# A macaron block (MoE, local attention, MoE): the experts' queues are no longer filled beforehand, and the first block's turning and the weights' splitting are moved

## The chip, the cores and the metric

The kernel runs on one core of one Trainium2 chip. A core has five engines, each with its own in-order list of instructions: TensorE (PE, matrix products, its weight loads shown as PEld), VectorE (DVE), ScalarE (ACT), GpSimd (POOL) and SyncE (SP, which here only issues transfers). Engines wait for one another, and for transfers, by semaphores; an instruction that waits holds up everything behind it on its engine. Sixteen DMA engines move data between DRAM and the on-chip memories SBUF and PSUM. The metric is the device time of one execution in microseconds, as the median of several runs.

## The reference

4096 tokens (2 x 2048) of width 256 go through three residual steps:

```
x = x + 0.5 * ffn(layernorm(x))
x = x + attention(layernorm(x))
x = x + 0.5 * ffn(layernorm(x))

def ffn(x):                             # 8 experts, 2 per token
    xn = x * rsqrt(mean(x*x) + eps)
    probs = softmax(xn @ router_w.T)
    topk_p, topk_i = top_k(probs, 2);  rw = topk_p / sum(topk_p)
    capacity = int(1.25 * 4096 / 8)     # 640
    # each expert takes its first 640 tokens, in the order of tokens
    dispatch = argsort(~sel, axis=1, stable=True)[:, :capacity]
    valid = arange(capacity) < count
    eout = (silu(xg @ rg) * (xg @ ru)) @ rd          # inner width 1024
    routed = zeros.at[dispatch].add(eout * (w * valid))
    shared = (silu(x @ sg) * (x @ su)) @ sd          # inner width 2048
    return shared + routed
```

The attention is causal within groups of 64 tokens, with 16 heads of width 16 and an RMS norm on q and k. With two experts per token the mean queue would be 1024 tokens long, so a queue of 640 places usually overflows, and tokens beyond its end are dropped.

## The kernel before

**Numbers in two halves.** Each product is made of three float16 products: value and weight are split into a high and a low half, and the lo x lo term is left out (`TERMS`). `split` (L97) makes the halves of a weight: a cast on ACT, then a subtraction on DVE. `two` (L161) does it for tokens.

**Four phases.** Phase a handles the tokens of the first ffn in 32 tiles of 128 (`tile1`): load y, statistics, normalise to z (`planes`, L146), write both halves into a row buffer X (ten of them), transpose into xb, compute router logits, and after each fourth tile route a block of 512 tokens (`route`, L214). Between these steps the shared expert is computed for blocks 0 to 4: `shared` (L349) goes through 16 chunks of the inner width, each with gate and up products (L306) into three PSUM buffers pgu, a Silu on ACT (L317), products on DVE (sl, L319), the halves hh (ACT, L321) and hl (DVE, L322), and the down products (L330), which are deferred past the next chunk's gate and up. Phase b computes the experts of the first ffn, phase c the rest of the first shared expert, the attention, and the second shared expert, and phase d the experts of the second ffn.

**Queues in DRAM.** `scatter` (L279) writes X, with a tag of token number and weights, by indirect transfers from POOL into the place that the token has in its expert's queue xg. Before that, `fill` (L742) writes zeros and a token number outside the range to all places: a memset on POOL, a small write on DVE and a transfer of 650 KB for each expert and each ffn, sixteen in all. All scatters of one ffn wait for its fills.

**Experts.** `experts` (L389) goes through 8 experts, with 8 chunks of weights each. For each chunk it loads re and re2, splits them into wc and wd, and computes gate and up for two stretches of columns, 384 and 256. `expert_load` (L373) brings the next expert's tokens (a transposing transfer) and tags; from the tag it makes eid, the token numbers as integers (a copy on POOL, L384), and ew, the weights (DVE, L385 and L387). After an expert's last chunk, `fin` scales the five tiles of output into eo, on DVE and ACT in turn, and POOL issues five indirect transfers that add them to the output rows named by eid (L426). They run while the next expert's first chunks are computed. eid, ew and tag have two buffers each, so those of expert e+2 take the place of those of expert e, and wait until its readers are done: for eid these are the five indirect transfers.

**What sets the order.** The program is written as generators: `drive` takes one step of the shared expert after another and lets the tiles take their steps in between; `run_slots` lets only the tiles run. The order in which the framework then lays the instructions out on each engine comes from a planner that simulates times while the program is built, so an edit can move instructions that it does not name. On the chip that order is fixed. SP issues nearly all plain and transposing transfers, one after another.

In phase a the first block is turned on TensorE (`turn`, L177), since no transposing transfer has to be waited for there; `front_steps` (L606) holds this. `load_shared` (L118) loads the shared expert's weights in eight pairs of chunks and splits them, all at one point of the program, after the first block's tiles.

Of the kernel before, what the change touches and what calls it, by code (L numbers as in the profile page):

```python
# [20 lines left out]
P = 128  # L21
# [8 lines left out]
E = 8  # L30
# [7 lines left out]
class Net:  # L38
    def __init__(self, ctx, tc):
# [27 lines left out]
        nc.gpsimd.memset(self.e1, 2.718281828459045)  # L67
        tk = self.sm.tile([P, 32], I32, name="tk", bufs=1)
# [35 lines left out]
    def load_router(self, router_w):  # L104
        nc = self.nc
        r = self.raw.tile([E, H], F32, name="rtr", tag="raw2")
# [11 lines left out]
    def load_shared(self, sg, su, sd):  # L118
# [5 lines left out]
        for c in range(0, 16, 2):  # L124
            r = self.raw.tile([P, 2, 2, 2 * P], F32, name=f"rs{c}", tag="raw")
            for i, s in enumerate((sg, su)):
                nc.sync.dma_start(
                    out=r[:, i], in_=s[:, c * P:(c + 2) * P].rearrange("(k p) f -> p k f", p=P))
            for j in range(2):
                src = r[:, :, :, j * P:(j + 1) * P]  # L130
                self.split(self.sgu[:, c + j, 0], self.sgu[:, c + j, 1], src)
            r2 = self.raw.tile([P, 2, H], F32, name=f"rd{c}", tag="raw2")
            nc.sync.dma_start(out=r2, in_=sd[c * P:(c + 2) * P].rearrange("(k p) f -> p k f", p=P))
            self.split(self.sdw[:, 0, c:c + 2], self.sdw[:, 1, c:c + 2], r2)

# [10 lines left out]
    def planes(self, x, xp, mv, rstd, pool=False):  # L146

        nc = self.nc
        z = self.tok.tile([P, H], F32, name="z", bufs=3)
# [8 lines left out]
        self.two(xp, z, pool)  # L158
# [55 lines left out]
    def route(self, R, b, fb):  # L214
# [33 lines left out]
        nc.vector.tensor_tensor(out=R["run"], in0=C[:, 3, :], in1=M[:, 3, :], op=ALU.add)  # L248
        yield
# [24 lines left out]
        for t in range(4):  # L274
            with self.tc.issue_after(self.anchor.ins) if self.anchor else nullcontext():
                self.scatter(R, b, fb, t, di, w1, dl, ef)
            yield

# [94 lines left out]
    def expert_load(self, R, e, hold):  # L373
# [10 lines left out]
        nc.gpsimd.tensor_copy(ids, tag[:, :, 0])  # L384
# [88 lines left out]
    def attn_tile(self, R, j, x2, new_fb):  # L473
# [12 lines left out]
        self.planes(y, xa, mv, rstd, True)  # L486
# [119 lines left out]
    def front_steps(self, y, t, new_fb, keep=None):  # L606
# [6 lines left out]
        z = self.planes(y, xp, fb["mv"][:, t, :], fb["rstd"][:, t:t + 1], keep is not None)  # L613
        xt = fb["xb"][:, :, t * P:(t + 1) * P]
        if fb["pe"]:
            self.turn(z, xt)
            fb["n"] += 1
            for _ in range((3 - t) * GAP_A + 1):
                yield
        if keep is not None:  # L620
# [16 lines left out]
class Tiles:  # L637
# [12 lines left out]
    def steps(self):  # L650
# [17 lines left out]
        self.slot += 1  # L668

# [27 lines left out]
def macaron(ctx, tc, x, w_qkv, ln_w, w_proj, router_w, rg, ru, rd, sg, su, sd, out):  # L697
# [24 lines left out]
    def tile1(j):  # L722
# [3 lines left out]
        yield  # L726
        yield from n.front_steps(y, t, new_fb(1, b))
# [14 lines left out]
    def fill(R):  # L742

        for e in range(E):
            z = n.raw.tile([P, 5, XW], F32, name="zero")
            nc.gpsimd.memset(z, 0.0)
            nc.vector.tensor_scalar_add(z[:, :, H], n.tokid[:, 0:5], float(T + e * CAP))
            nc.sync.dma_start(out=R["xg"][e * CAP:(e + 1) * CAP].rearrange("(t p) f -> p t f", p=P), in_=z)
            yield

# [75 lines left out]
```

## Time and profile before

| What | Value |
|---|---|
| Median of 3 runs | 1871.48 us (1870.2 to 1871.99) |
| Profiled execution, its own time | 1875.79 us |
| Its span in the profile | 1874.1 us |
| Granted TensorE clock, mean | 0.994 |
| Instructions | 37396 |
| Transfers | 196.07 MB, mean 105 GB/s |

In the profile a row of the time order has start, duration, engine, line, operation, output<-inputs, size, and in brackets the idle time before it with what ended it. A row of groups has busy time and mean duration, and the idle time ahead. A row of waits has who waited for whom, total us, times and the longest. TensorE's busy time counts matmuls from issue to modelled end, and neighbours overlap: in the experts' phases six matmuls of 128 x 384 take 0.98 us. The costliest lines are these:

```profile
L306 PE MATMUL pgu<-xb,sgu 128*128 128x512 f16 x3072 | 738.8, 380 | 26.3 <-DVE sl L319 11.1
L306 PE MATMUL pgu<-xe,wc 128*128 128x384 f16 (+1 forms) x3072 | 497.0, 299 | 0.5
L426 POOL DMA_INDIRECT out_dram<-eo,eid x40 | 64.6, 1616 | 313.8 <-DVE hl L322 248.3
L287 POOL DMA_INDIRECT xg<-X,di x128 | 136.0, 1063 | 112.2 <-DVE di L266 54.1
```

### The profile page before, as it was taken

To read this page: it belongs to the slowest core of one execution; us is meant where nothing else is said; L and a number is where in the kernel's file an instruction comes from. 1 tells how busy PE (TensorE), PEld (TensorE's weight loads), DVE (VectorE), ACT (ScalarE), POOL (GpSimd) and SP (SyncE) were. 2 spreads that over 40 slices of the span, in tenths; PEclk is the share of its full clock that TensorE was granted. 3 is DMA by queue.
4 is the path that set the end of the run, shared out by engine and by line. 5 is a ranking of instruction groups with operands and counts; after the bars stand their busy time and mean duration, and the time that the engine had idled before them with its cause. 6 is when DMAs were issued, how large, how long until landed. Compare 5 with 4: busy or idle time off the path is not lost.

```text
span 1874.1 us, 37396 instructions
## 1 busy us (share of the span) xinstructions
PE 1786.8 (95%) x13546; PEld 1191.7 (64%) x13546; DVE 1262.5 (67%) x3190; ACT 942.1 (50%) x1991; POOL 724.5 (39%) x943
## 2 busy tenths in 40 slices
PE   6899999999999999999999999999999999999996
PEld 3455555677777765666565655656566567777775
DVE  8756554456666656788888888888886556565663
ACT  5323323355555535666566666656643335555553
POOL 5743332011112223455757667575753001111122
PEclk9999999999999999999999999999999999999998
DMA  9742113045455424556657576766631304544542
GB/s 278 220 125 75 35 29 86 21 102 115 112 113 125 104 55 86 110 105 120 139 114 141 102 141 119 135 121 119 129 62 37 86 12 102 114 113 105 117 109 50
DMA packets 447481, 196.07 MB, mean 105 GB/s; under 512 B 302353, under 2 KB 444365, under 8 KB 447248
## 3 DMA queue, kind: packets, MB, share of 16 engines
q1 hardware_dynamic: 429632, 172.51, 41.1%
q0 software_dynamic: 17664, 21.17, 6.6%
q8 instruction: 106, 1.74, 0.4%
q14 instruction: 79, 0.65, 0.1%
HBM read 80.52 MB, written 52.33 MB: 71 GB/s over the span
## 4 chain that ended last, share of the span: by engine, by line
PE 57%; DVE 12%; POOL 10%; issue 9%; DMA 6%; ACT 4%; SPq 2%; POOLq 0%; DVEq 0%; ACTq 0%
PE pgu L306 36%; PE po L330 19%; POOL xg L287 3%; DVE hl L322 2%; DVE sl L319 2%; DVE sl L314 2%; DMA xg<-X,di 1%; DMA QT<-QK 1%; DMA rs<-in_L_ffn_su_dram 1%; POOL X L285 1%; DMA y<-in_L_attn_x_dram 1%; ACT hh L321 1%; POOL e L561 1%; DVE st L139 1%; POOL S L550 1%
## 5 line engine op out<-in xcount | busy, mean ns | idle before, releaser
L306 PE MATMUL pgu<-xb,sgu 128*128 128x512 f16 x3072 | 738.8, 380 | 26.3 <-DVE sl L319 11.1
L321 ACT CAST hh<-sl 128x512 f16<-128x512 f32 (+2 forms) x512 | 272.8, 533 | 563.3 <-DVE sl L319 521.4
L306 PE MATMUL pgu<-xe,wc 128*128 128x384 f16 (+1 forms) x3072 | 497.0, 299 | 0.5
L306 PEld LDWEIGHTS <-sgu 128*128 128x128 f16 x3072 | 293.2, 98 | 301.1 <-issue 35.8
L319 DVE SCALAR_TENSOR_TENSOR sl<-pgu,sl 128x512 f32<-128x512 f32 (+2 forms) x512 | 300.2, 587 | 204.7 <-PE pgu L306 171.4
L322 DVE TENSOR_TENSOR hl<-sl,hh 128x512 f16<-128x512 f32 (+2 forms) x512 | 328.4, 642 | 154.4 <-ACT hh L321 147.5
L330 PEld LDWEIGHTS <-hh 128*128 128x128 f16 x3328 | 320.6, 98 | 115.0 <-ACT hh L321 17.9
L306 PEld LDWEIGHTS <-wc 128*128 128x128 f16 x3072 | 300.5, 98 | 94.1 <-issue 1.8
L330 PE MATMUL po<-sdw,hh 128*128 128x256 f16 x2048 | 351.9, 273 | 7.3 <-ACT hh L321 6.9
L330 PE MATMUL po<-sdw,hl 128*128 128x256 f16 x1024 | 251.9, 274 | 15.8 <-DVE hl L322 10.8
L330 PE MATMUL po<-wd,hh 128*128 128x256 f16 x1280 | 223.4, 273 | 0.0
L330 PEld LDWEIGHTS <-hl 128*128 128x128 f16 x1664 | 162.9, 98 | 67.4 <-DVE hl L322 27.2
L317 ACT ACTIVATE sl<-pgu 128x384 f32<-128x384 f32 (+1 forms) x336 | 159.0, 473 | 55.3 <-PE pgu L306 34.2
L426 POOL DMA_INDIRECT out_dram<-eo,eid x40 | 64.6, 1616 | 313.8 <-DVE hl L322 248.3
L287 POOL DMA_INDIRECT xg<-X,di x128 | 136.0, 1063 | 112.2 <-DVE di L266 54.1
L426 POOL DMA_INDIRECT acc<-eo,eid x40 | 65.1, 1627 | 285.4 <-DVE hl L322 245.8
L330 PE MATMUL po<-wd,hl 128*128 128x256 f16 x640 | 152.4, 273 | 2.1 <-DVE hl L322 2.1
L314 DVE SCALAR_TENSOR_TENSOR sl<-sl,pgu 128x512 f32<-128x512 f32 x176 | 119.9, 681 | 38.3 <-ACT sl L313 37.2
L100 ACT ACTIVATE wc<-re 128x512 f16<-128x512 f32 x128 | 80.5, 629 | 83.3 <-PE pgu L306 52.9
L313 ACT ACTIVATE sl<-pgu 128x512 f32<-128x512 f32 x176 | 103.9, 591 | 33.3 <-PE pgu L306 31.8
L101 DVE SCALAR_TENSOR_TENSOR wc<-re,wc 128x512 f16<-128x512 f32 x128 | 88.3, 690 | 26.6 <-ACT wc L100 26.4
L550 POOL TENSOR_TENSOR S<-S,amx 128x1024 f32<-128x1024 f32 x32 | 63.7, 1990 | 81.3 <-DVE amx L549 74.4
(140 smaller groups left out, 1719.6 us busy)
## 6 DMA issues: line engine op xcount, KB each, us to landing
re<-in_L_ffn_rg_dram SPq DMA_DIRECT2D x128, 128.0 KB
re<-in_L_ffn_ru_dram SPq DMA_DIRECT2D x128, 128.0 KB
re<-in_L_ffn_rd_dram SPq DMA_DIRECT2D x128, 128.0 KB
xg<-zero SPq DMA_DIRECT2D x16, 650.0 KB
y<-acc SPq DMA_DIRECT2D x64, 128.0 KB
y<-in_L_attn_x_dram SPq DMA_DIRECT2D x32, 128.0 KB
acc<-xr SPq DMA_DIRECT2D x16, 256.0 KB
x<-y SPq DMA_DIRECT2D x32, 128.0 KB
```

The costliest lines, as they stand in the source:

```text
L101: nc.vector.scalar_tensor_tensor(out=lo, in0=src, scalar=WS, in1=hi, op0=ALU.mult, op1=ALU.subtract)
L287: i = nc.gpsimd.indirect_dma_start(out=R["xg"][:, :], out_offset=bass.IndirectOffsetOnAxis(ap=di[:, t, k:k + 1], axis=0), in_=X, in_offset ...
L306: nc.tensor.matmul(p, lhsT=wc[:, w, i, k, :], rhs=x[:, 2 * a + k, :], start=(j == 0), stop=(j == 5))
L313: nc.scalar.activation(s, p, AF.Tanh, scale=0.5 / XP)
L314: nc.vector.scalar_tensor_tensor(out=s, in0=s, scalar=1.0, in1=p, op0=ALU.add, op1=ALU.mult)
L317: nc.scalar.activation(s, p, AF.Silu, scale=1.0 / XP)
L319: nc.vector.scalar_tensor_tensor(out=s, in0=ps[1], scalar=1.0 / XP / (2.0 * XP if tanh else 1.0), in1=s, op0=ALU.mult, op1=ALU.mult)
L321: nc.scalar.copy(h[0], s)
L322: nc.vector.tensor_tensor(out=h[1], in0=s, in1=h[0], op=ALU.subtract)
L330: nc.tensor.matmul(o, lhsT=h[a][:, t * P:(t + 1) * P], rhs=wd[:, w], start=(c == 0 and j == 0 and t % 2 == 0), stop=(c == nch - 1 and j == 2),
L426: i = nc.gpsimd.indirect_dma_start(out=R["acc"][:, :], out_offset=bass.IndirectOffsetOnAxis(ap=ids[:, t:t + 1], axis=0), in_=eo, in_offset ...
L550: self.anchor = nc.gpsimd.tensor_tensor(out=S, in0=S, in1=mx.unsqueeze(2).to_broadcast([P, 16, 64]), op=ALU.subtract)
```

## The change

- `fill` is gone for both ffns. Places that no token took hold whatever the memory held. After the last block is routed, `limits` sums the queues' counts over all partitions with one matmul, and makes two small tables: a mask of bits and an offset for each place of each queue. In `expert_load`, eid is made on DVE: the tag's bits are masked, and 8192 is added for places that were not taken, so that the adding transfer skips them. The copy on POOL is gone.
- `acc` for blocks 5 to 7 is no longer copied from x in DRAM by three transfers of 512 KB; each tile's y is written from SBUF, 128 KB at a time.
- `planes` is divided into `normed` and `two`. In the first block, the turning comes first and `two` (the halves for the scatter) later. z has five buffers instead of three.
- The shared expert's weights have four buffers of each kind instead of two. Their loads and splits are written as a generator: the first pair is loaded at the start, from ACT's queue, and split when the first block is ready; the others are loaded and split one pair in every six steps of the first block (`fed`).
- A small Silu at the start loads ACT's function table.
- `load_router`'s buffer is its own.

```diff
--- before.py
+++ after.py
@@ -65,6 +65,8 @@
         nc.gpsimd.memset(self.mhalf, -0.5)
         self.e1 = c.tile([P, 4], F32, name="e1")
         nc.gpsimd.memset(self.e1, 2.718281828459045)
+        warm = c.tile([P, 8], F32, name="warm")
+        nc.scalar.activation(warm, self.mhalf, AF.Silu)
         tk = self.sm.tile([P, 32], I32, name="tk", bufs=1)
         nc.gpsimd.iota(tk, pattern=[[P, 32]], base=0, channel_multiplier=1)
         self.tokid = c.tile([P, 32], F32, name="tokid")
@@ -103,7 +105,7 @@
 
     def load_router(self, router_w):
         nc = self.nc
-        r = self.raw.tile([E, H], F32, name="rtr", tag="raw2")
+        r = self.raw.tile([E, H], F32, name="rtr", bufs=1)
         nc.sync.dma_start(out=r, in_=router_w)
         self.rwt = self.cst.tile([P, 2, 2 * E], F16, name="rwt")
         p = self.m1([P, 2, E], F32, "prt")
@@ -122,16 +124,20 @@
         self.sgu = w.tile([P, 16, 2, 2, 2, P], F16, name="sgu")
         self.sdw = w.tile([P, 2, 16, H], F16, name="sdw")
         for c in range(0, 16, 2):
-            r = self.raw.tile([P, 2, 2, 2 * P], F32, name=f"rs{c}", tag="raw")
+            issue = nc.sync if c else nc.scalar
+            r = self.raw.tile([P, 2, 2, 2 * P], F32, name=f"rs{c}", tag="raw", bufs=4)
             for i, s in enumerate((sg, su)):
-                nc.sync.dma_start(
+                issue.dma_start(
                     out=r[:, i], in_=s[:, c * P:(c + 2) * P].rearrange("(k p) f -> p k f", p=P))
+            r2 = self.raw.tile([P, 2, H], F32, name=f"rd{c}", tag="raw2", bufs=4)
+            issue.dma_start(out=r2, in_=sd[c * P:(c + 2) * P].rearrange("(k p) f -> p k f", p=P))
+            if c == 0:
+                yield
             for j in range(2):
                 src = r[:, :, :, j * P:(j + 1) * P]
                 self.split(self.sgu[:, c + j, 0], self.sgu[:, c + j, 1], src)
-            r2 = self.raw.tile([P, 2, H], F32, name=f"rd{c}", tag="raw2")
-            nc.sync.dma_start(out=r2, in_=sd[c * P:(c + 2) * P].rearrange("(k p) f -> p k f", p=P))
             self.split(self.sdw[:, 0, c:c + 2], self.sdw[:, 1, c:c + 2], r2)
+            yield
 
     def stats(self, x, mv, rstd):
         nc = self.nc
@@ -143,10 +149,10 @@
             out=ve, in0=mv[:, 1:2], scalar1=LN_EPS, scalar2=1.0 / UP ** 2, op0=ALU.add, op1=ALU.mult)
         nc.gpsimd.tensor_tensor(out=rstd, in0=ve, in1=self.mhalf[:, :1], op=ALU.pow)
 
-    def planes(self, x, xp, mv, rstd, pool=False):
-
-        nc = self.nc
-        z = self.tok.tile([P, H], F32, name="z", bufs=3)
+    def normed(self, x, mv, rstd, pool=False):
+
+        nc = self.nc
+        z = self.tok.tile([P, H], F32, name="z", bufs=5)
         if pool:
             nm = self.sm.tile([P, 1], F32, name="nm")
             nc.vector.scalar_tensor_tensor(
@@ -155,7 +161,6 @@
         else:
             nc.vector.tensor_scalar(
                 out=z, in0=x, scalar1=mv[:, 0:1], scalar2=rstd, op0=ALU.subtract, op1=ALU.mult)
-        self.two(xp, z, pool)
         return z
 
     def two(self, xp, z, pool=False):
@@ -246,6 +251,9 @@
         for t in range(3):
             nc.vector.tensor_tensor(out=C[:, t + 1, :], in0=C[:, t, :], in1=M[:, t, :], op=ALU.add)
         nc.vector.tensor_tensor(out=R["run"], in0=C[:, 3, :], in1=M[:, 3, :], op=ALU.add)
+        if b == NB - 1:
+            yield
+            self.limits(R)
         yield
         pp = self.m1([P, 4, E], F32, "pp")
         nc.tensor.matmul(pp, lhsT=self.tri, rhs=M, start=True, stop=False)
@@ -275,6 +283,21 @@
             with self.tc.issue_after(self.anchor.ins) if self.anchor else nullcontext():
                 self.scatter(R, b, fb, t, di, w1, dl, ef)
             yield
+
+    def limits(self, R):
+
+        nc = self.nc
+        p = self.m1([P, E], F32, "pn")
+        nc.tensor.matmul(p, lhsT=self.ones, rhs=R["run"], start=True, stop=True)
+        taken = self.sm.tile([P, E, 5], F32, name="taken", bufs=1)
+        nc.vector.tensor_tensor(
+            out=taken, in0=self.tokid[:, 0:5].unsqueeze(1).to_broadcast([P, E, 5]),
+            in1=p.unsqueeze(2).to_broadcast([P, E, 5]), op=ALU.is_lt)
+        R["bits"] = self.cst.tile([P, E, 5], I32, name=R["key"] + "b")
+        nc.vector.tensor_scalar_mul(R["bits"], taken, -1.0)
+        R["off"] = self.cst.tile([P, E, 5], F32, name=R["key"] + "o")
+        nc.vector.tensor_scalar(
+            out=R["off"], in0=taken, scalar1=-8192.0, scalar2=8192.0, op0=ALU.mult, op1=ALU.add)
 
     def scatter(self, R, b, fb, t, di, w1, dl, ef):
         nc = self.nc
@@ -381,7 +404,9 @@
         yield
         ids = hold["id"] = self.sm.tile([P, 5], I32, name="eid")
         w = hold["w"] = self.sm.tile([P, 5], F32, name="ew")
-        nc.gpsimd.tensor_copy(ids, tag[:, :, 0])
+        tk = self.sm.tile([P, 5], I32, name="tkb")
+        nc.vector.tensor_tensor(out=tk, in0=tag[:, :, 0].bitcast(I32), in1=R["bits"][:, e], op=ALU.bitwise_and)
+        nc.vector.tensor_tensor(out=ids, in0=tk.bitcast(F32), in1=R["off"][:, e], op=ALU.add)
         nc.vector.scalar_tensor_tensor(
             out=w, in0=tag[:, :, 3], scalar=float(e), in1=tag[:, :, 1], op0=ALU.is_equal, op1=ALU.mult)
         nc.vector.tensor_tensor(out=w, in0=w, in1=tag[:, :, 2], op=ALU.add)
@@ -483,7 +508,7 @@
         self.stats(y, mv, rstd)
         yield
         xa = a.tile([P, 2 * H], F16, name="xa")
-        self.planes(y, xa, mv, rstd, True)
+        self.two(xa, self.normed(y, mv, rstd, True), True)
         yield
         V2 = self.V2[j % 2]
         xt = self.flip(xa)
@@ -610,13 +635,14 @@
         X = self.xs.tile([P, XW], F32, name="X")
         xp = X[:, 0:H].bitcast(F16)
         fb["X"][t] = X
-        z = self.planes(y, xp, fb["mv"][:, t, :], fb["rstd"][:, t:t + 1], keep is not None)
+        z = self.normed(y, fb["mv"][:, t, :], fb["rstd"][:, t:t + 1], keep is not None)
         xt = fb["xb"][:, :, t * P:(t + 1) * P]
         if fb["pe"]:
             self.turn(z, xt)
             fb["n"] += 1
             for _ in range((3 - t) * GAP_A + 1):
                 yield
+        self.two(xp, z, keep is not None)
         if keep is not None:
             self.nc.sync.dma_start(out=keep, in_=y)
         yield
@@ -668,6 +694,14 @@
         self.slot += 1
 
 
+def fed(main, weights):
+
+    for i, _ in enumerate(main):
+        if i % 6 == 0:
+            next(weights, None)
+        yield
+
+
 def run_slots(tiles, until):
     while not until():
         for _ in tiles.steps():
@@ -724,6 +758,8 @@
         y = n.load_tile(x, b, t)
         yield
         yield
+        if b >= NA:
+            nc.sync.dma_start(out=R1["acc"][j * P:(j + 1) * P], in_=y)
         yield from n.front_steps(y, t, new_fb(1, b))
         yield from tail(R1, 1, b, t)
 
@@ -739,31 +775,19 @@
         yield from n.shared(b, fbs[key]["xb"], src, dst, **k)
         used.add(key)
 
-    def fill(R):
-
-        for e in range(E):
-            z = n.raw.tile([P, 5, XW], F32, name="zero")
-            nc.gpsimd.memset(z, 0.0)
-            nc.vector.tensor_scalar_add(z[:, :, H], n.tokid[:, 0:5], float(T + e * CAP))
-            nc.sync.dma_start(out=R["xg"][e * CAP:(e + 1) * CAP].rearrange("(t p) f -> p t f", p=P), in_=z)
-            yield
-
     with n.phase("a", BT, 2, 10):
         n.ident = n.at.tile([P, P], F32, name="ident")
         make_identity(nc, n.ident)
+        weights = n.load_shared(sg, su, sd)
+        next(weights)
         n.load_router(router_w)
         tiles = Tiles(tile1, 32, GAP_A)
         run_slots(tiles, ready(1, 0))
-        n.load_shared(sg, su, sd)
-        for _ in fill(R1):
-            pass
+        next(weights)
         for b in range(NA):
             run_slots(tiles, ready(1, b))
-            if b == 2:
-                tiles.extra.append(fill(R2))
-                for i in range(NA, NB):
-                    nc.sync.dma_start(out=R1["acc"][i * BT:(i + 1) * BT], in_=x[i * BT:(i + 1) * BT])
-            drive(all_shared((1, b), b, x, R1["acc"]), tiles, RATE_A)
+            main = all_shared((1, b), b, x, R1["acc"])
+            drive(fed(main, weights) if b == 0 else main, tiles, RATE_A)
         run_slots(tiles, tiles.done)
         cur = {}
         for _ in n.expert_load(R1, 0, cur):
```

## Prediction

> **What bounds the kernel now.** The page first: busy time per engine, and the chain that ended last.
>
> ```profile
> PE 1786.8 (95%) x13546; PEld 1191.7 (64%) x13546; DVE 1262.5 (67%) x3190; ACT 942.1 (50%) x1991; POOL 724.5 (39%) x943
> ...
> PE 57%; DVE 12%; POOL 10%; issue 9%; DMA 6%; ACT 4%; SPq 2%; POOLq 0%; DVEq 0%; ACTq 0%
> ```
>
> TensorE is the bound, so an edit counts only by the TensorE idle time that it makes or removes. Then the stages, in windows of time (window, length, busy us of each engine, granted clock, DMA share, GB/s): loading and first block, rest of phase a, seven experts, and the last stretch with eight.
>
> ```profile
> 0.00:60.00 60.00, 42.86 (x254) 23.79 (x255) 49.80 (x186) 30.67 (x59) 32.08 (x76) 0.97 1.02 282
> 60.00:340.00 280.00, 262.91 (x1666) 155.06 (x1665) 153.06 (x541) 86.22 (x156) 111.89 (x207) 0.99 0.30 81
> 340.00:680.00 340.00, 339.59 (x2654) 259.35 (x2652) 200.56 (x428) 174.06 (x406) 58.67 (x41) 1.00 0.43 97
> ```
>
> In the first 60 us the DMA engines are full (1.02, 282 GB/s) and TensorE is idle for 17 us. In 60 to 340 it is idle for 17 more. The experts' stretch has 0.4 us idle in 340: nothing to win there, and all to lose.
>
> **Part 1: fills gone, y copied from SBUF.** Removed: 16 memsets on POOL (1.18 us each), 16 small DVE writes (0.15) and 16 transfers of 650 KB, the last issued at 105.9 us. They hold TensorE up indirectly. The chain shows "DMA xg<-zero" for 8.36 us at 52.65, then the first scatters at 65.28; casts into X wait 14.5 us on ACT for a buffer that such a scatter holds (waits up to 160 us), and a cast blocks the hh behind it. TensorE's gaps of over 0.7 us between 56 and 106 are 1.34, 0.92, 1.97, 1.02, 1.99: 7.2 us. At 144.6 a gap of 2.5 and at 139.4 one of 1.1 end after DVE waited 3.1 us for a late y load; with five z buffers and loads ahead of the transposes in SP's order that should go too: 3.6 us. Two half-clock spells (below) follow these gaps, 1.7 each. Possible gain: 7.2 + 3.6 + 3.4 = 14.2 us. The acc copies (12 of 128 KB for 3 of 512 KB) make SP wait for each y load; SP idles 107.8 to 133.1, which covers it. Without that cover y comes late again: 2.5 us a time.
>
> **Part 2: the first block.** In the built program ACT and DVE are in order, and the splits of all eight weight pairs stand ahead of the first hh cast on ACT, six ahead of the first Silu. The data up to there are 8 x 0.79 MB weights, 11 tiles of 0.13 and xr 0.52: 8.2 MB, at 282 GB/s 29 us after the first landing at about 3; plus 2 us of casts: TensorE runs freely from 34 us. By then it has made seven groups of six gate/up matmuls at 1.31: 9.2 us of work. Before, it had 18 matmuls (3.9 us) by 24.3, then 9.7 us less one half-clock spell: 11.9. So 3 us behind, and one more spell, 1.7: I take +4, from 0 (DMA at the 340 to 380 GB/s of single stretches) to +9 (no overlap). The saved table load (1.28 us before the first Silu at 22.35) and the earlier turning of z drown in this wait. Phase a together: -14.2 + 4 = **-10**, from -16 to +5.
>
> **Part 3: queue ids move from POOL to DVE.** Each expert's eid was one POOL copy (0.19 us); it becomes an AND and an ADD on VectorE. At about 0.17 us each (the row of ew, same tile) 32 of them are 5 us on an engine that is 59% busy among experts: nothing by itself. But eid has two buffers. The id list of expert e+2 overwrites that of e, which expert e's five scattered adds read, so the write waits until they have landed. POOL did this waiting; nothing was queued behind it that mattered. All waits of POOL, two rows (total us, times, longest), then POOL and DVE in order of time at the first such place:
>
> ```profile
> POOL eid L384 <- DMA acc<-eo,eid: 17.5, 6, 4.2
> ...
> POOL eid L384 <- DMA out_dram<-eo,eid: 14.2, 5, 3.4
> ```
> ```profile
> 413.64 1.88 POOL L426 DMA_INDIRECT acc<-eo,eid  x1 [0.30 <-DVE sl L319]
> 417.99 0.29 POOL L384 CAST eid<-tag 128x5 int32<-128x5 f32 x1 [2.46 <-DMA acc<-eo,eid]
> ```
> ```profile
> 413.11 0.42 DVE L319 SCALAR_TENSOR_TENSOR sl<-pgu,sl 128x256 f32<-128x256 f32 x1
> 413.44 0.68 DVE L101 SCALAR_TENSOR_TENSOR wc<-re,wc 128x512 f16<-128x512 f32 x1
> 414.04 0.42 DVE L101 SCALAR_TENSOR_TENSOR wd<-re,wd 128x256 f16<-128x256 f32 x1
> 414.38 0.41 DVE L322 TENSOR_TENSOR hl<-sl,hh 128x256 f16<-128x256 f32 x1
> 414.76 0.56 DVE L319 SCALAR_TENSOR_TENSOR sl<-pgu,sl 128x384 f32<-128x384 f32 x1
> ```
>
> The changed program's order on VectorE at this place (place, line, operation, waits):
>
> ```
> 720 L342 sl_5115<-pgu_5117,sl_5115 128x256
> 721 L409 eid_5208<-tkb_5210,scatter0o_3779 [waits DMASW3 DMASW4 DMASW2 DMASW1]
> 722 L408 tkb_6344<-tag_6208,scatter0b_3777
> 723 L103 wc_5220, 724 L103 wd_5150, then hl_5088, sl_5162
> ```
>
> So eid stands between the sl of 413.11 and the wc of 413.44. VectorE gets there at 413.11 + 0.42 = 413.5 and waits until 418.0: 4.5 us. Behind it wait wc, wd, hl and sl, and TensorE for them:
>
> ```profile
> 416.67 0.27 PE L330 MATMUL po<-wd,hl 128*128 128x256 f16 x1
> 416.78 0.27 PE L330 MATMUL po<-wd,hh 128*128 128x256 f16 x1
> 416.89 0.27 PE L330 MATMUL po<-wd,hl 128*128 128x256 f16 x1
> 417.00 1.14 PE L306 MATMUL pgu<-xe,wc 128*128 128x384 f16 x6
> ```
>
> The po at 416.67 needs that hl; the pgu at 417.00 needs the PSUM buffer that the sl of 414.76 frees. Once eid may run at R, DVE does eid and tkb (0.35), then wc, wd, hl at their own spacing (1.32 from wc to sl), then sl 0.56: freed at R + 2.3 with the handover. 417.99 + 2.3 - 417.00 = 3.3 us of TensorE idle. ACT's next Silu follows before TensorE asks for it, so nothing is added later; TensorE has no slack to win it back.
>
> This repeats for experts 2 to 7 in both expert phases, at the same relative place. In all twelve the pgu stands 3.48 us after VectorE's arrival, so each loses its wait less 1.2. From POOL's eid times and VectorE's sl ends: 418.0-413.5, 457.5-452.8, 497.0-492.2, 536.4-531.5, 576.5-570.8, 616.8-610.2, 1593.9-1589.1, 1634.1-1629.8, 1674.3-1669.1, 1713.3-1709.6, 1754.4-1748.9, 1794.0-1788.3: 60.4 us of waiting; less 12 x 1.18: **46.3 us** of TensorE. Lower bound: the Trainium skill's "DMA: Bandwidth & Descriptors", section Anatomy of one DMA, gives about 2.0 us as a transfer's fixed cost, while these scatters landed 2.9 and 2.8 us after issue on average (17.5 / 6, 14.2 / 5). With 2.0 the sum would be 46 - 12 x 0.85 = 36; I take the rows, which are of the same transfers.
>
> **Part 4: the clock after the stalls.** Windows of the trace (PEclk is the third number from the end): a gap of TensorE, then the 3.4 us after it; first a gap of 1.99 us, last one of 1.97.
>
> ```profile
> 103.70:105.60 1.90, 0.00 (x0) 0.00 (x0) 1.14 (x5) 0.01 (x1) 1.18 (x1) 1.00 1.02 346
> 106.50:109.90 3.40, 3.36 (x15) 1.79 (x13) 3.33 (x30) 0.49 (x2) 1.58 (x6) 0.51 1.02 303
> ...
> 79.30:82.70 3.40, 3.22 (x21) 1.88 (x22) 3.33 (x19) 0.89 (x2) 2.73 (x12) 1.00 0.69 225
> ```
>
> The three longest gaps after the start (3.75, 2.51, 1.99) were each followed by a spell at half clock, none shorter was. A spell costs 1.7 us of work. The Trainium skill's "TensorE: Matmul & The Clock Gate", section HAM oscillation — how this bites in real kernels, asks only that there be no idle gaps over about 3.4 us; the new main gaps are 2.2 to 5.2 us, seven above that: 7 x 1.7 = 12 us. By the row all twelve count: 12 x 1.7 = **20.5 us**. I take the row, since a gap of 2.0 already cost a spell here.
>
> **Part 5: limits and the handovers between phases.** Two small matmuls (as pp, 0.18 us), six small DVE operations and a step more before the last scatters; in return wc of the first expert stands one hh later on ACT, and eid's wait for tag is shared with ew. The tags of experts 2 and 3 are now awaited on DVE there. Between -2 and +4; I take +1. Phase c keeps its order, apart from these.
>
> **Sum.** -10 + 46.3 + 20.5 + 1 = +58. The profiled execution took 1875.79 us (span 1874.1), so 1934 for such a one; against the median of the runs, 1871.48, it makes **1930 us**.
>
> **Rivals.** (1) The stalls come but the clock mostly holds: 1930 - 20 = 1910. For it: the gap of 1.97 at 77.3 and one of 1.91 at 684.9 cost no clock, and the expert stretch is dense around each gap. Against: the three longer ones. (2) The front-loaded splits spoil the first block and the later gaps stay, since X still waits for scatters (phase a +3 instead of -10): 1943. For it: ACT's order; against: the DMA share of 0.30 after 60 us. (3) Faster: VectorE doesn't wait, because the scatters have landed when it reaches eid. Then only phase a is left: 1871.5 - 10 + 1 = 1862.5, at best 1856. It decides at eid's place on VectorE: landing would have to come at least 3.6 us earlier at every expert (the smallest of the twelve waits), or at least some 4 us earlier on average to bring the loss under phase a's gain. Nothing in the change moves the scatters earlier. (4) The fills were hidden anyway: phase a 0, 1940, inside the range.
>
> **How the numbers follow.** Main case 0.60; (1) 0.20; (2) and (4) together 0.15; (3) 0.05, of which a little lies within 0.2% of before, which is about what a measurement can tell from no change. The range leaves out (3) and the tails: low end from (1) with DMA landings at the shorter value, 1900; high end from (2) with a little more, 1947.
>
> **What would show it.** In the changed profile: eid on VectorE with about 5 us idle ahead of it, ended by the scattered adds, twelve times, 60 us in all; TensorE gaps of 2 to 5 us behind each, and half-clock spells after them; experts' stretches longer by some 33 us each; phase a ending some 10 us sooner, without the gaps of 56 to 147 us but with a Silu at 25 us or later. I am wrong if VectorE's waits for these adds are under 1 us each, or if TensorE's gaps are much shorter than VectorE's waits less 1.2.

## The result, and the profile after

The changed kernel takes 1903.1 us (median of four, 1903.0 to 1906.8) where the kernel before takes 1870.8 (1868.9 to 1872.0): a ratio of 1.018, 95% interval 1.0167 to 1.0193, so 32 us slower. Forecast were 1930 us, from 1900 to 1947, so the result lies near the lower end. The profiled execution took 1906.75 us (span 1905.0), 31.0 more than the one of before.

The busy times of the page, and then the same stages as before in windows of time (window, length, busy us of PE, PEld, DVE, ACT and POOL, granted clock, DMA share, GB/s):

```profile
PE 1797.7 (94%) x13548; PEld 1194.7 (63%) x13548; DVE 1259.1 (66%) x3212; ACT 939.8 (49%) x1991; POOL 704.4 (37%) x911
```
```profile
0.00:60.00 60.00, 42.36 (x254) 23.69 (x255) 50.17 (x189) 30.43 (x60) 28.30 (x73) 1.00 0.60 176
60.00:340.00 280.00, 275.50 (x1782) 165.06 (x1781) 153.42 (x537) 91.13 (x165) 98.12 (x192) 1.00 0.26 66
340.00:680.00 340.00, 323.53 (x2502) 246.13 (x2501) 192.89 (x424) 165.92 (x394) 56.79 (x35) 0.98 0.43 97
```

Two things happened at once. Phase a got better: from 60 to 340 us TensorE is idle for 4.5 us where it was 17.1, and the DMA share of the first 60 us fell from 1.02 to 0.60. The experts' stretch got worse: 16.5 us idle where it was 0.4, and the clock is at 0.98. A share of 94% for 95% hides both.

VectorE's waits, the rows of eid (total us, times, longest), and VectorE in order of time at the first place:

```profile
DVE eid L409 <- DMA acc<-eo,eid: 26.1, 6, 4.6
DVE eid L409 <- DMA out_dram<-eo,eid: 25.3, 6, 4.8
```
```profile
394.08 0.42 DVE L342 SCALAR_TENSOR_TENSOR sl<-pgu,sl 128x256 f32<-128x256 f32 x1
398.44 0.17 DVE L409 TENSOR_TENSOR eid<-tkb,scatter0o 128x5 int32<-128x5 f32 x1 [3.94 <-DMA acc<-eo,eid]
398.64 0.17 DVE L408 TENSOR_TENSOR tkb<-tag,scatter0b 128x5 int32<-128x5 int32 x1
398.75 0.69 DVE L103 SCALAR_TENSOR_TENSOR wc<-re,wc 128x512 f16<-128x512 f32 x1
399.36 0.42 DVE L103 SCALAR_TENSOR_TENSOR wd<-re,wd 128x256 f16<-128x256 f32 x1
399.69 0.42 DVE L345 TENSOR_TENSOR hl<-sl,hh 128x256 f16<-128x256 f32 x1
400.03 0.55 DVE L342 SCALAR_TENSOR_TENSOR sl<-pgu,sl 128x384 f32<-128x384 f32 x1
```

The wait that GpSimd used to do is now on VectorE, twelve times, 51.4 us in all, between that sl and that wc. TensorE behind it, in order of time, and then its waits for hl in the two expert phases (340 to 640 us, 1540 to 1840 us):

```profile
396.99 0.82 PE L329 MATMUL pgu<-xe,wc 128*128 128x256 f16 x6
400.17 0.28 PE L353 MATMUL po<-wd,hl 128*128 128x256 f16 x1 [2.36 <-DVE hl L345]
...
400.63 1.35 PE L329 MATMUL pgu<-xe,wc 128*128 128x384 f16 x6
```
```profile
PE po L353 <- DVE hl L345: 16.3, 6, 3.0
...
PE po L353 <- DVE hl L345: 16.5, 7, 3.1
```

The first matmul that starves is the po that needs the hl of 399.69. The twelve gaps, added one by one, are 31.8 us of idle time (1.36 to 3.10 each). Nine of them are followed by a spell of half clock. Two of the gaps in windows of 3.41 us each: first the gap of 2.36 us and the window after it, which runs at half clock; then the gap of 2.74 us of the next expert, which lies across two windows, and the window after it, at full clock:

```profile
397.99:401.40 3.41, 1.23 (x8) 0.79 (x9) 2.35 (x7) 0.79 (x3) 0.00 (x0) 1.00 0.19 56
401.40:404.81 3.41, 3.41 (x15) 1.81 (x13) 1.92 (x5) 1.51 (x5) 0.00 (x0) 0.50 0.44 139
438.94:442.36 3.42, 2.38 (x22) 1.85 (x19) 0.03 (x1) 0.00 (x0) 1.05 (x1) 1.00 0.56 72
442.36:445.77 3.41, 1.71 (x12) 1.14 (x13) 2.80 (x8) 1.26 (x4) 0.00 (x0) 1.00 0.30 90
445.77:449.18 3.41, 3.41 (x31) 2.77 (x29) 2.53 (x6) 1.94 (x6) 0.00 (x0) 1.00 0.43 132
```

The account between the two profiled executions: phase a, TensorE's idle time 34.2 to 22.1 us up to 340 us, and its three half-clock spells gone (half of a window of 3.41 us, 1.7 us each): -17.2. The experts' gaps: +31.8. Nine spells: +15.3. The end of phase c, where a gap of 1.27 us became one of 2.63 and a spell: +3.1. Together +33.0, against 31.0 between those executions and 32.3 between the medians.

### The profile page after: what moved, and what is told of

The parts are those of the page before. It is cut to its first block, busy times and chain, and to the rows that moved or that the text cites. A ratio compares the mean times of both kernels' runs of the same rounds, so it can differ in the third digit from the quotient of the medians.

```text
span 1905.0 us, 37349 instructions
## 1 busy us (share of the span) xinstructions
PE 1797.7 (94%) x13548; PEld 1194.7 (63%) x13548; DVE 1259.1 (66%) x3212; ACT 939.8 (49%) x1991; POOL 704.4 (37%) x911
## 5 line engine op out<-in xcount | busy, mean ns | idle before, releaser
L329 PE MATMUL pgu<-xb,sgu 128*128 128x512 f16 x3072 | 736.5, 380 | 17.2 <-DVE sl L337 9.0
L329 PE MATMUL pgu<-xe,wc 128*128 128x384 f16 (+1 forms) x3072 | 508.0, 304 | 0.3
L353 PE MATMUL po<-wd,hh 128*128 128x256 f16 x1280 | 227.8, 277 | 0.0
```

Source lines behind the costliest of these rows:

```text
L329: nc.tensor.matmul(p, lhsT=wc[:, w, i, k, :], rhs=x[:, 2 * a + k, :], start=(j == 0), stop=(j == 5))
L353: nc.tensor.matmul(o, lhsT=h[a][:, t * P:(t + 1) * P], rhs=wd[:, w], start=(c == 0 and j == 0 and t % 2 == 0), stop=(c == nch - 1 and j == 2),
```

## Experiments

The chips on which these ran differ a little: the kernel before took 1869.1, 1869.3 and 1869.8 us beside most of them, and 1877.0 beside e4_fills, e5_acc, e6_weights and e8_limits. Where runs of different chips are set side by side, the ratio to the kernel before is used. The edits are cut to their main lines, and "..." marks what is left out between them.

### Taking the wait away: eight lists, then four

```diff
-        ids = hold["id"] = self.sm.tile([P, 5], I32, name="eid")
+        ids = hold["id"] = self.sm.tile([P, 5], I32, name="eid", bufs=8)
```

> The changed kernel with eight buffers for eid instead of two, so that no expert's list is written over one that scattered adds still read; eid stays on VectorE, with its AND and ADD. Theory (VectorE's wait for the landings is what costs the time in both expert phases): the twelve waits of 51.4 us are gone, TensorE's gaps of 1.4 to 3.1 us in the expert phases and the nine half-clock spells behind them too; in the windows of TensorE's lost time these phases cost 23.4 + 23.5 = 46.9 us more than before, so 1903.1 - 46.9 = 1856 us, from 1852 to 1860, and faster than the kernel before by some 15 us. Rival (the loss is from the extra VectorE instructions, the counts and the masks, or from the new order at the phases' ends): within 5 us of the changed kernel, 1898 to 1908.

Measured: 1857.1 us (1855.8 to 1857.5), ratio 0.9937, interval 0.992 to 0.9953. No wait of eid for a scattered add is left. The window 340 to 650 us, for this kernel; the experts' products start at 341 to 343 us in it and in the changed kernel and at 361 in the kernel before, and go on past 650 in all three; TensorE was busy for 309.59 us of it in the kernel before and 293.53 in the changed one, here for 309.56:

```profile
340.00:650.00 310.00, 309.56 (x2456) 239.95 (x2455) 189.83 (x417) 163.74 (x388) 56.75 (x35) 1.00 0.48 107
```

So one argument of one tile is worth 1.0180 - 0.9937 = 2.4%, 45.5 us, and with it gone the rest of the change is a gain. The rival, that the extra instructions, counts or masks cost the time, is out: they are all still there.

With four buffers instead of eight:

> The same with four buffers. The program's order keeps eid at the same four places of each expert phase for experts 4 to 7, since it is made as soon as a buffer is free by the order; only experts 2 and 3 lose their wait. So four of the twelve stalls are gone. Theory: a third of 46.9 us less than the changed kernel: 1903.1 - 15.6 = 1887.5 us, from 1882 to 1892; VectorE waits for the adds eight times, some 34 us. Rival (a stall is paid once a phase, by a shift of the transfers or of the clock that later ones share): 1900 to 1904. Second rival (two buffers more are enough, as a count of buffers would suggest): 1856.

Measured: 1885.5 us (1884.4 to 1886.0), ratio 1.0089, interval 1.0072 to 1.0106. VectorE's rows:

```profile
DVE eid L409 <- DMA out_dram<-eo,eid: 11.5, 4, 3.1
DVE eid L409 <- DMA acc<-eo,eid: 11.2, 4, 3.1
```

Eight waits are left, as the order of the program said. From eight buffers to four is 28.4 us for eight stalls, 3.6 each; the twelve of the changed kernel cost 45.5, 3.8 each. The price of one hardly depends on how many there are, so the stalls add up one by one. The waits came out shorter than expected (22.7 for 34), since the tkb ahead of eid now takes part of them (21.3 us of waits for the tags, 11.5 in the changed kernel). Four buffers were not enough because the order is made by when a buffer is free in it: with more buffers eid is made for a later expert, and still stands at the landing of the adds that free its buffer.

### The engine alone

```diff
-        nc.gpsimd.tensor_copy(ids, tag[:, :, 0])
+        nc.vector.tensor_copy(ids, tag[:, :, 0])
```

> The kernel before with one word changed: the copy that makes eid runs on VectorE instead of GpSimd. The fills stay, there are no counts and masks, the loads stay as they were. Theory: the stall comes with the engine alone, so 1870.8 + 46.9 = 1918 us, from 1910 to 1925, with twelve VectorE waits for the adds of some 50 us. Rival (the mask's instructions or the new phase a bring it about): 1869 to 1874.

Measured: 1911.0 us (1908.2 to 1912.3), ratio 1.0227, interval 1.021 to 1.0244. In the kernel before, one word makes it 42 us slower, with nothing else of the change in it:

```profile
DVE eid L384 <- DMA acc<-eo,eid: 26.0, 6, 4.4
DVE eid L384 <- DMA out_dram<-eo,eid: 25.2, 6, 4.7
```

51.2 us in twelve waits, as in the changed kernel (51.4). The two experiments meet: taking the wait out of the changed kernel gains 45.5 us, putting it into the kernel before loses 42.

### Handing the wait back to GpSimd

```diff
-        nc.vector.tensor_tensor(out=ids, in0=tk.bitcast(F32), in1=R["off"][:, e], op=ALU.add)
+        fd = self.sm.tile([P, 5], F32, name="fid")
+        nc.vector.tensor_tensor(out=fd, in0=tk.bitcast(F32), in1=R["off"][:, e], op=ALU.add)
+        nc.gpsimd.tensor_copy(ids, fd)
```

> The changed kernel with the wait handed back to GpSimd: VectorE makes the masked list as floats in a tile of its own, and a GpSimd copy turns it into eid (two buffers as before). Theory: VectorE no longer stands at the landings; GpSimd waits some 3 us at the same twelve places with nothing behind it that TensorE needs: 1856 us, as with eight buffers, at most 1860. Rival (VectorE is held anyway, since its own tile is free only once GpSimd has copied two experts earlier): the wait comes back, over 1880.

Measured: 1893.0 us (1892.3 to 1896.2), ratio 1.0132, interval 1.0115 to 1.0149. I expected 1856; the rival was right. VectorE's waits for fid, then GpSimd's for eid:

```profile
DVE fid L410 <- POOL eid L411: 24.2, 8, 3.2
```
```profile
POOL eid L411 <- DMA acc<-eo,eid: 17.1, 6, 4.1
POOL eid L411 <- DMA out_dram<-eo,eid: 16.3, 6, 3.4
```

GpSimd does wait at the twelve places. But fid has two buffers as well, so VectorE may not write a fid until GpSimd has copied the one of two experts before, and that copy stands at the landing: a wait handed on through a short ring comes back. In the kernel before, the ring behind GpSimd's eid is the tag, which a DMA queue fills, so no compute engine stood there.

### What phase a gained, and from what

First each part undone in the changed kernel with eight lists (ratio 0.9937). The fills put back, with the masks kept, so that they are useless work:

```diff
         next(weights)
+        for _ in fill(R1):
+            pass
         for b in range(NA):
...
+            if b == 2:
+                tiles.extra.append(fill(R2))
             main = all_shared((1, b), b, x, R1["acc"])
```

> The changed kernel with eight eid buffers, and both sets of fills put back at their old places (the masks stay, so the fills are useless work). Against 1857.1 for eight buffers without the fills. Theory of the prediction (the fills hold the scatters and so the X buffers, 7.2 us of gaps with the clock spells behind them): 1857 + 9 = 1866 us, from 1863 to 1870. Rival (the fills were hidden, and the 18 us of phase a come from the weights' and y's new order): 1855 to 1859.

Measured: 1863.4 us, ratio 0.9926, interval 0.9909 to 0.9942: no loss. Beside this run and the next two, e8_limits (below, 1864.2 us on the same chip) is the nearest measure, since it has all these parts as in the changed kernel. The fills are not harmless where they run: of the stretch from 40 to 80 us TensorE is busy for 34.95 us at a clock of 0.92, where e8_limits, which has the same phase a without fills and ran on the same chip, has 38.98 at 1.00:

```profile
40.00:80.00 40.00, 34.95 (x213) 20.54 (x213) 32.27 (x137) 13.06 (x26) 31.75 (x52) 0.92 0.81 210
80.00:340.00 260.00, 252.76 (x1624) 150.00 (x1623) 141.23 (x485) 83.22 (x150) 92.31 (x176) 1.00 0.28 75
```

Of the 7.2 us lost there (4.0 of idle time, 3.2 of clock), 4.8 come back around it: up to 40 us it has 26.65 us of TensorE work for 24.26, and from 80 us on 252.76 for 250.31. Why the first block runs earlier with the fills in the order was not tried.

The acc copies as before:

```diff
-        if b >= NA:
-            nc.sync.dma_start(out=R1["acc"][j * P:(j + 1) * P], in_=y)
...
+            if b == 2:
+                for i in range(NA, NB):
+                    nc.sync.dma_start(out=R1["acc"][i * BT:(i + 1) * BT], in_=x[i * BT:(i + 1) * BT])
```

> The changed kernel with eight eid buffers, and the residual of blocks 5 to 7 copied as before: three transfers of 512 KB from DRAM to DRAM at the third block instead of twelve of 128 KB from the y tiles. Theory (the late y loads of 139 to 147 us are cured by five z buffers and by the order of the queue, not by this): 1857 to 1859 us. Rival (the y loads were late because they stood behind these large transfers): two gaps, 3.6 us, and a half-clock spell of 1.7 come back, 1862.

Measured: 1865.4 us, ratio 0.9941, interval 0.9925 to 0.9958: nothing, as expected.

The weights as before (two raw buffers, all pairs loaded and split by one call after the first block's tiles):

```diff
-        weights = n.load_shared(sg, su, sd)
-        next(weights)
         n.load_router(router_w)
...
-        next(weights)
+        n.load_shared(sg, su, sd)
```

> The changed kernel with eight eid buffers, and the shared experts' weights loaded and split as before (two raw buffers, after the first block's tiles, no pair ahead of use). Theory of the prediction (the front-loaded splits cost the first block 4 us): 1853 us, from 1850 to 1856. Rival (fetching the weights in pairs is where a part of phase a's gain comes from, since the splits no longer stand among the first block's hh casts): the start is some 2 us better and the stretch from 20 to 60 us some 5 to 8 us worse, 1860 to 1865.

Measured: 1863.7 us, ratio 0.9927, interval 0.991 to 0.9943. The 4 us that I expected lie within the two intervals, and this kernel's own runs spread from 1861.4 to 1867.3, so this run settles nothing.

z as before (three buffers, its halves split in the same step):

```diff
-        z = self.tok.tile([P, H], F32, name="z", bufs=5)
+        z = self.tok.tile([P, H], F32, name="z", bufs=3)
...
-        z = self.normed(y, fb["mv"][:, t, :], fb["rstd"][:, t:t + 1], keep is not None)
+        z = self.planes(y, xp, fb["mv"][:, t, :], fb["rstd"][:, t:t + 1], keep is not None)
...
-        self.two(xp, z, keep is not None)
```

> The changed kernel with eight eid buffers, and the normalised tile z handled as before: three buffers for five, its two halves split off in the same step, ahead of the first block's turn. Putting back fills, acc copies or weights, each alone, left the ratio to the kernel before where eight buffers have it (0.9926, 0.9941, 0.9927 beside 0.9937), so this is the one part of phase a not yet undone. Theory (z is what carries phase a's gain): some 10 us of it lost, ratio 0.998 to 1.001. Rival (the parts stand in for each other; no single one carries it): 0.992 to 0.9955.

Measured: 1858.6 us, ratio 0.9935, interval 0.9918 to 0.9951: nothing, and my theory here (z is the part that is left, so it carries the gain) fell. No single part, undone by itself, takes the gain away. So the other way round, each part alone in the kernel before. No fills (with the counts and masks in their place, and eight lists on VectorE):

```diff
-        for _ in fill(R1):
-            pass
...
-                tiles.extra.append(fill(R2))
...
+        if b == NB - 1:
+            yield
+            self.limits(R)
```

> The kernel before without its fills, with the counts and masks that stand in for them and eight eid buffers on VectorE; weights, z and acc copies stay. With the fills put back into the changed kernel, the stretch from 40 to 80 us lost 8.9 us of TensorE instead of 2.4, though the sum hardly moved. Theory (the fills' 6.5 us come off, and the masks' step costs some 3 at the end of the third phase): ratio 0.997 to 0.999. Rival 1 (no fills is the whole gain of phase a): 0.9925 to 0.995. Rival 2 (without the other parts it gains nothing): 1.000 to 1.002.

Measured: 1853.5 us (1852.5 to 1855.1), ratio 0.9913, interval 0.9896 to 0.993. This is the fastest kernel of the study, 15.8 us under the one before, and about 50 under the changed one by the ratios. My own expectation (0.997 to 0.999) was wrong, rival 1 was right: leaving out the fills is the whole gain, and a little more. The run takes in the masks and the eight lists on VectorE too, but its gain is made in phase a: up to 340 us TensorE is idle for 19.0 us, where the kernel before is idle for 34.2 and has three half-clock spells. The stages up to 40, 80 and 340 us:

```profile
0.00:40.00 40.00, 27.82 (x147) 14.06 (x148) 34.09 (x124) 24.27 (x48) 16.49 (x49) 1.00 0.97 273
40.00:80.00 40.00, 38.05 (x255) 23.40 (x254) 29.36 (x125) 14.64 (x27) 23.97 (x50) 1.00 0.27 70
80.00:340.00 260.00, 255.16 (x1651) 152.88 (x1650) 140.64 (x481) 84.81 (x152) 87.14 (x166) 1.00 0.23 59
```

Against the kernel with eight lists, on the same chip (24.43, 38.82 and 257.41 us of TensorE work), it is 3.4 us ahead by 40 us and gives back all but 0.4 of it by 340. In time it is 3.6 us ahead (1853.5 for 1857.1, and the two ranges don't meet; the intervals of the ratios just overlap), or 1.8 between the profiled executions. So once the fills are gone, weights, z and acc copies together gain nothing; what they cost beyond the 0.4 us is not placed by these traces.

The z part alone:

```diff
-        z = self.tok.tile([P, H], F32, name="z", bufs=3)
+        z = self.tok.tile([P, H], F32, name="z", bufs=5)
...
+        self.two(xp, z, keep is not None)
         if keep is not None:
```

> The kernel before with the z part alone: five buffers, split after the turn; fills, weights, acc copies and eid on GpSimd stay. Theory (z carries phase a's gain): ratio 0.992 to 0.995. Rival (it needs the others): 0.998 to 1.001.

Measured: 1865.1 us, ratio 0.9978, interval 0.9968 to 0.9988: 4 us, just under the rival's bound. The weights part alone, with all fills in place:

```diff
+        weights = n.load_shared(sg, su, sd)
+        next(weights)
         n.load_router(router_w)
...
-        n.load_shared(sg, su, sd)
+        next(weights)
         for _ in fill(R1):
...
+            drive(fed(main, weights) if b == 0 else main, tiles, RATE_A)
```

> The kernel before with the weights part alone: pairs in four buffers, loaded ahead of the first tiles and split a pair ahead of use; fills, z, acc copies and eid on GpSimd stay. Known: without fills the kernel before is at 0.9913 (so the fills cost it some 16 us), but putting the fills back beside the new weights, z and acc copies costs next to nothing (0.9926 beside 0.9937). Theory (the fills do harm by making the next weight pairs late: ScalarE waits 6.75 us for a pair that lands at 20.9 us; with the pairs loaded ahead they find nothing to make late): ratio 0.992 to 0.996. Rival (the other parts, z and the acc copies, do it; or the front-loaded splits take back what the early pairs give): 0.998 to 1.002.

Measured: 1860.9 us (1860.6 to 1862.1), ratio 0.9953, interval 0.994 to 0.9967: 9 us, as the theory had it. ScalarE's waits for the raw weights between 10 and 60 us, first the kernel before, then this one (total, times, longest):

```profile
ACT sgu L100 <- DMA rs<-in_L_ffn_su_dram: 13.5, 6, 6.8
```
```profile
ACT sgu L100 <- DMA rs<-in_L_ffn_su_dram: 2.2, 2, 1.2
```

So the parts stand in for each other. Taking the fills away helps by 16 us, loading and splitting the pairs in the new way by 9 with the fills still there, and whoever has one of the two finds the other worth little or nothing. That the fills do their harm by making the pairs late, as the theory of this run has it, is not shown. Without the fills these waits are still most of what they were:

```profile
ACT sgu L100 <- DMA rs<-in_L_ffn_su_dram: 9.6, 5, 4.2
```

And of the 10.1 us of idle time that TensorE loses less with the new weights up to 340 us, 7.4 are saved after 80 us, when these waits are over; first the kernel before, then this one:

```profile
80.00:340.00 260.00, 246.94 (x1563) 145.55 (x1562) 138.00 (x480) 80.84 (x145) 95.17 (x180) 0.99 0.28 75
```
```profile
80.00:340.00 260.00, 254.34 (x1631) 151.90 (x1632) 141.33 (x479) 83.75 (x150) 94.09 (x182) 0.99 0.26 70
```

By which waits the fills cost the kernel before its 16 us stays open.

### The handover at the end of phase c

```diff
-        if b == NB - 1:
-            yield
-            self.limits(R)
...
                 self.scatter(R, b, fb, t, di, w1, dl, ef)
+            if t == 3 and b == NB - 1:
+                self.limits(R)
             yield
```

> The changed kernel with eight eid buffers, and the counts and masks made behind the last scatters instead of in a step of their own ahead of the last positions. Theory (that step makes the last scatters, the gather and the tags of the first experts later, so that VectorE and ScalarE stand at late loads in the last two chunks of the shared expert: a TensorE gap of 2.73 us at 1461.7 with a half-clock spell, where the kernel before had 1.27 and none): 3 us less, 1854 us, from 1852.5 to 1855.5, and that gap under 1.6 us. Rival (the order of the loads at the phase's end does it, not the step): 1856 to 1858, the gap stays.

Measured: 1864.2 us, ratio 0.9935, interval 0.9918 to 0.9952: no difference that can be told from 0.9937. Forty microseconds around the handover in the kernel before, with eight lists, and with the masks made last:

```profile
1447.00:1487.00 40.00, 38.35 (x234) 22.46 (x233) 23.56 (x40) 12.91 (x24) 8.68 (x10) 1.00 0.41 95
```
```profile
1440.00:1480.00 40.00, 36.06 (x212) 20.93 (x210) 21.58 (x45) 12.39 (x22) 5.90 (x6) 0.96 0.43 100
```
```profile
1437.00:1477.00 40.00, 38.05 (x225) 22.23 (x224) 23.47 (x50) 12.71 (x23) 6.41 (x7) 0.96 0.44 99
```

In the profile 2.0 of the 2.3 us of idle time come back, so the extra step is where most of that loss was; the gap of 2.73 us became one of 1.95, not under 1.6 as expected, and its half-clock spell stayed. The step's place is shown by the trace; a gain in time is not.

## Why the prediction was right, and where its sum was off

**Sign and mechanism (Part 3): right.** The wait sits where the prediction put it, between that sl and that wc, twelve times, with po and pgu behind it; eight lists remove it, and one word brings it into the kernel before. Its size was off, and mostly by the waits: 51.4 us, not 60.4. I took the landings as the rows of before have them. There eid follows the start of the last add by 4.56 us on average over the twelve places, in the changed kernel by 3.91. Most of that comes from the last two experts of each phase (5.2 and 3.9 us); one of them, before and then after:

```profile
610.78 1.73 POOL L426 DMA_INDIRECT acc<-eo,eid  x1 [0.30 <-DVE wc L101]
616.75 0.19 POOL L384 CAST eid<-tag 128x5 int32<-128x5 f32 x1 [4.24 <-DMA acc<-eo,eid]
```
```profile
612.77 1.54 POOL L451 DMA_INDIRECT acc<-eo,eid  x1 [0.30 <-issue]
616.63 0.17 DVE L409 TENSOR_TENSOR eid<-tkb,scatter0o 128x5 int32<-128x5 f32 x1 [4.39 <-DMA acc<-eo,eid]
```

In e3_pool, where VectorE does not stand at the last two experts, these landings take 5.0 to 5.7 us again; why they are slower there was not tried.

What a wait costs TensorE was forecast well in the prediction's own measure, which is how much later the pgu starts. At the first place it starts 3.64 us after the pgu ahead of it (400.63 and 396.99), and in the kernel before 0.98 (417.00, and the row below), so it is 2.66 late for a wait of 3.94:

```profile
416.02 0.82 PE L306 MATMUL pgu<-xe,wc 128*128 128x256 f16 x6
```

Over the twelve places that makes 35.7 us, the wait less 1.31 each, for the 1.18 forecast. So 46.3 stands beside 35.7, at the lower bound of 36. The bound's transfer of about 2.0 us (an estimate by the Trainium skill's "DMA: Bandwidth & Descriptors", Anatomy of one DMA) was nearer than the 2.9 and 2.8 of the rows: eid follows the end of the last issue by 2.37 us on average. The 31.8 of the account are less still, because the profile counts a matmul as busy until its modelled end, 397.81 at the first place, which is after the next one would have been issued (0.65 us behind the pgu in the kernel before, so at 397.64), and because the pgu then comes 0.46 us behind that po and not 0.33: the sl that frees its buffer ends at 400.58, the second thing that the prediction had it wait for.

**The clock (Part 4): right that it comes, 15.3 us for 20.5.** By the rule that I weighed, gaps over about 3.4 us (the Trainium skill's "TensorE: Matmul & The Clock Gate", HAM oscillation — how this bites in real kernels), there should have been no spell at all, since the longest gap is 3.10; there were nine. By my row, by which a gap of 2.0 is enough, eleven of the twelve should have had one. (Seven forecast gaps above 3.4 us was a slip: the twelve waits less 1.18 give 2.5 to 5.4 us, nine of them above it. The sum took the row and is not touched.) Neither rule holds; the last section has what the traces show.

**Phase a (Parts 1 and 2): -17.2 for -10.** The idle time fell by 12.1 us. Three spells went and none came, where two were forecast to go and one to come: the one at 24.5 us went too. Of the idle time, 3.4 us are gaps after 160 us, which I hadn't counted, as I took only those of over 0.7 us up to 147. The first 160 and the last 180 us of phase a, in the changed kernel (131.40 and 174.38 us of TensorE work before):

```profile
0.00:160.00 160.00, 140.04 (x892) 81.82 (x893) 113.30 (x436) 63.35 (x122) 75.93 (x167) 1.00 0.44 126
160.00:340.00 180.00, 177.83 (x1145) 106.93 (x1143) 90.29 (x291) 58.21 (x103) 50.49 (x98) 1.00 0.20 50
```

Part 1's size, 14.2, stands beside 15.8 measured without the fills, and that is in part luck: the gaps went, but not by the path that it gave. ScalarE's waits of the casts into X for scatters, from 40 to 340 us, before and after, did not go:

```profile
ACT X L164 <- DMA xg<-X,di: 25.4, 14, 3.0
```
```profile
ACT X L169 <- DMA xg<-X,di: 30.2, 18, 3.1
```

Part 2 was right that the front-loaded splits come first: the first hh cast runs at 29.64 us, behind the splits of all eight pairs, where it ran at 25.44 before. Its cost of 4 us is seen at the start, where by 40 us the kernel with eight lists has 3.4 us less TensorE work than the one with only the fills gone; by 340 us all but 0.4 of it is made up. Part 2 had no such making up.

**The handovers (Part 5): +3.1 for +1**, inside the range given. I had put the step ahead of the last scatters into it, but not that a gap there brings a spell of its own.

**Rivals.** (1), 1910, is nearest in time, and for the wrong reason: the clock did not hold, the stalls were shorter. (2) and (4) failed on phase a. (3), the faster one, needed landings before VectorE's arrival; they came 2.9 to 4.8 us after it.

In the account of idle time and clock, the errors of phase a, of Part 3 and of Part 4 have one sign, 7.2, 14.5 and 5.2 us too dear; less the 2.1 of Part 5 they make 24.8 of the 27 us between 1930 and 1903.

## What to carry to other kernels

Before an instruction is moved to another engine, ask what it waits for, not what it costs: 0.17 us of VectorE work brought a wait of 4 us with it, because the tile that it writes is free only when the transfers that read it have landed. Give such a tile as many buffers as there are lists: a ring of four for eight lists took only four of the twelve waits away here, since the order made eid earlier. And undo the parts of a change both ways, out of the new kernel and into the old one: two parts that each gain alone look worthless when each is taken out beside the other.

## What the runs showed of the hardware that was not expected

The clock gate. The starts of all half-clock spells within one kernel lie whole multiples of 3.413 us apart, so there is a grid of such windows that runs on by itself; the Trainium skill says the same of its length ("TensorE: Matmul & The Clock Gate", What's actually happening), and the trace agrees. The length of a gap does not tell whether a spell follows: in the fourteen profiled kernels of this case, from 21 to 1838 us, there are 57 gaps of TensorE of 2.00 us or more, and 15 had none behind them. How much of a single window of this grid is idle tells it better, counting gaps over 0.25 us: all 43 windows with 2.00 us or more of idle time were followed by one window at half clock, and of some 155 with 1.00 to 1.99 us only twelve were, one of them under 1.40. Nine of the twelve lie at one place, near 960 to 1000 us, with 1.40 to 1.70 us idle; why a spell follows there is not known, and in e4_fills one more came after a window with 0.96, itself at half clock. The 2.00 was read from the same traces that it is counted on, so it is a description and not a tested limit. In the windows shown at the start, the gap of 2.36 us at 397.81 lies almost whole in one window (2.18 of 3.41 idle) and costs 1.7 us; the longer one of 2.74 at 441.3 is cut by a window's edge into 1.04 and 1.70, and costs nothing. So a stall of 2 to 3 us pays the clock or not by where it falls, and windows with less than 1.40 us idle were nearly all free of it.

The chips: the same kernel before took 1869 to 1870 us on two of them and 1877 on a third, 0.4% more, so differences of that size mean something only against a run on the same chip.
